# Local attention on one Trainium2 core: both key tiles of half a batch's heads in one slot

## The chip, the cores and the metric

The kernel runs on one core of one Trainium2 chip. The metric is the device time of one execution in microseconds (us), as the median of several runs. A core has TensorE (PE in the profile; PEld is its weight load), VectorE (DVE), ScalarE (ACT), GpSimd (POOL) and SyncE (SP, which issues transfers). Each engine works through its own instructions in the order in which the program issues them, and waits on semaphores for the others. Matmul results land in PSUM, which has eight banks; each bank holds 512 float32 values in each of 128 partitions.

## The reference

The whole model is a chain of sixteen blocks on a tensor of 16 x 256 tokens with 128 channels. The change touches one of them, which is used twice (second and fourth block) and has two layers, so its attention loop runs four times. What one layer computes, cut to its core:

```python
def _layer(x, wqkv, qs, ksc, wo, lg, lb, w1, b1, w2, b2):
    h = shift_token(x)
    q, k, v = jnp.split(h @ wqkv, 3, axis=-1)
    q, k, v = (to_heads(q), to_heads(k), to_heads(v))      # 8 heads of 64
    q = l2norm(q) * qs
    k = l2norm(k) * ksc
    q, k = rotary_xpos(q, k)
    o = local_attention(q, k, v)                           # windows of 64, one window back
    x = x + o @ wo
    h = shift_token(x)
    h = (h - mu) / jnp.sqrt(var + 1e-05) * lg + lb
    ...                                                    # gated feed-forward, added to x

def local_attention(q, k, v):
    ...
    sim = jnp.einsum('bhwid,bhwjd->bhwij', bq * QK_SCALE, bk)
    mask = (i < j) | (i > j + WINDOW) | (j == -1)
    sim = jnp.where(mask, -jnp.finfo(sim.dtype).max, sim)
    attn = jax.nn.softmax(sim, axis=-1)
    return jnp.einsum('bhwij,bhwjd->bhwid', attn, bv)
```

A key is seen by at most the queries of its own and the next 64 positions. With 256 tokens in two key tiles of 128, the first key tile needs 192 queries, the second 128.

## The kernel before

`local_layer` calls `local_attend` (the loop that changes) and then `local_ffn`. The four calls of `local_attend` are called loops 1 to 4 here; loops 1 and 3 are the first layer of each block, loops 2 and 4 the second. The transfers in flight during loop 1 bring weights for later stages.

Tokens are cut into 32 tiles of 128 (`NTILE`, two for each of 16 batches) and into 8 chunks of 512 (`NCH`). A unit of attention is one batch `b`, one half of the heads `hg` and one key tile `t`, which makes 64 units. The order of work is written out by hand (`manual_schedule`): slot `k` handles unit `k`, and the steps for tiles and chunks are placed at fixed offsets from it. Two slots, an even one with t = 0 and an odd one with t = 1, make one pair; a pair also takes one token tile through each of its steps. In every engine the instructions stand in the order in which the slot calls its steps.

The steps, with what each puts on the engines:

- `project` (L3385): two 128x512 matmuls for queries and keys into two banks; ACT squares each (`sq`), DVE multiplies each by the cosine and the sine table (`t1`, `t2`, four multiplies).
- `rotate` (L3403): DVE sums the squares (`ss`) and takes a maximum with a small number; POOL adds the rotated halves, two instructions.
- `unit` (L3413): ACT takes the inverse root by Ln and Exp, POOL multiplies by it (1.90 us).
- `turn` (L3421): eight transposes into two banks, which ACT copies to `qkt`, and the matmul for the values, which ACT copies to `v`.
- `score` (L3436): for t = 0, four 64-row products of 192 columns, clipped by DVE with a minimum against the table `see`, then one Exp over 768 columns (L3462). For t = 1, two mask matmuls in bf16 (an identity times the mask, started first), then four products of 128 columns added to them, then two Exp of 256 columns from PSUM (L3454).
- `weigh` (L3465), two slots later: the sums of the weights (`ones64`, into bank `pd`) and the weighted values (two halves, into bank `po`), in four column groups of 32. With t = 1, ACT forms the inverse of the sums by Ln and Exp (`rd`).
- `divide` (L3491): DVE multiplies `po` by `rd` into `ot`.
- `out` (L3501), for each chunk: four 128x512 matmuls and an addition to `z` by DVE.
- `chunk_steps` (L3514): a layer norm for each chunk in three steps (centre: matmul, ACT copy, POOL square; spread: matmul, ACT Ln and Exp; scale: DVE L543 and ACT with a bias), the shift by one token (three POOL instructions), and in the first layer the norm of `x` for those chunks that the stage before has not normed already (three of eight).

PSUM is shared as w = 3 banks (projections, turns, values, output, norms), s = 2 (scores) and o = 3 (sums). A float32 matmul is issued as two passes, so counts in the profile are twice those above. In the profile, `ps` is any PSUM bank, `w,hb` the projections, values and, after the loop, the feed-forward, `ct` the constants (identity, ones, mean matrices), and `pt` the attention weights.

## Time and profile before

| what | value |
|---|---|
| median of three runs | 4373.4 us (4373.02 to 4376.56) |
| the profiled execution | 4392.96 us |
| its span in the profile | 4391.2 us |
| granted TensorE clock over the span | 0.952 of full |
| first scores of loops 1 to 4 begin at | 140.9, 519.5, 1198.8, 1577.7 us |
| start of loop 2's first score to start of its last | 519.5 to 778.7 us |
| ACT rows `pt<-pt` 128x768 (the wide Exp) | 0.84 us each, 128 of them |
| DVE rows `pt<-ps,w` 128x384 (the minimum) | 0.55 us each, 256 of them |

A time in the profile is counted from the start of the span. "Busy" is the time in which an engine has an instruction in flight; for PE the end of a matmul is modelled, so consecutive matmuls overlap in the rows, and the starts say more than the durations. In a row of the timeline the first number is the start, the second the time until the last of a merged group ends, and the bracket holds the idle time of the engine before it and what ended it. A wait is put down to the one that came last.

### The profile page before, as it was taken

What the parts mean: (1) busy time and instruction counts of PE and PEld (TensorE: products, weight loads), DVE (VectorE), ACT (ScalarE), POOL (GpSimd) and SP (SyncE); (2) the same over time, 40 slices, a digit from 0 to 9 for tenths busy, and PEclk for the clock granted to TensorE, in tenths of its full rate; (3) what the DMA queues carried; (4) which work ended last, traced back from release to release, by engine and by line L of the source; (5) the groups of instructions that cost most, each with busy time, mean ns of one, the idle gap of its engine ahead of it and who ended that gap; (6) DMA issues with size and microseconds to landing.
All of it is one profiled execution on the core that took longest, in us unless ns stands there. A gap on an engine that the chain in (4) does not pass through costs nothing. (4 is left out here: it accounts for less than half of the span.)

```text
span 4391.2 us, 72802 instructions
## 1 busy us (share of the span) xinstructions
PE 3966.2 (90%) x28390; PEld 2202.4 (50%) x28390; DVE 2605.3 (59%) x4455; ACT 2376.1 (54%) x4549; POOL 2119.4 (48%) x1776
## 2 busy tenths in 40 slices
PE   7899999999899999995989969887999899899978
PEld 3455455466355445543975549643333344355333
DVE  4764566364366377456336643564888788386374
ACT  6665466444766456553447634445555554675442
POOL 4653355232455255315433334466998789521251
PEclk8999999999999999997999979998999999999989
DMA  1800000000000000001940029200000000000000
GB/s 59 332 1 1 11 1 1 19 1 1 19 1 1 1 3 1 1 0 49 310 162 10 15 88 326 86 18 16 1 1 1 3 1 1 15 2 18 6 0 20
DMA packets 78400, 176.36 MB, mean 40 GB/s; under 512 B 12606, under 2 KB 39108, under 8 KB 77920
## 3 DMA queue, kind: packets, MB, share of 16 engines
q1 hardware_dynamic: 65568, 148.40, 9.8%
q0 software_dynamic: 9120, 18.51, 1.2%
q8 instruction: 227, 3.72, 0.4%
q10 hardware_dynamic: 3360, 4.72, 0.3%
q14 instruction: 125, 1.02, 0.1%
HBM read 118.28 MB, written 54.20 MB: 39 GB/s over the span
## 5 line engine op out<-in xcount | busy, mean ns | idle before, releaser
L528 ACT ACTIVATE pt<-ps 128x512 f32<-128x512 f32 (+1 forms) x896 | 423.1, 537 | 408.1 <-PE ps L504 406.8
L504 PE MATMUL ps<-hb,w 128*128 128x512 f32 (+1 forms) x960 | 468.9, 623 | 5.4 <-issue 3.3
L531 DVE TENSOR_TENSOR t<-ps,tab 128x512 f32<-128x512 f32 x512 | 319.3, 683 | 196.1 <-ACT sq L528 191.3
L504 PE MATMUL ps<-w,hb 128*128 128x512 f32 (+2 forms) x896 | 415.1, 576 | 13.6 <-DVE t L531 11.3
L534 POOL TENSOR_TENSOR t<-t,ss 128x1024 f32<-128x1024 f32 x128 | 243.7, 1904 | 306.8 <-ACT ss L528 197.7
L534 POOL TENSOR_TENSOR t<-t,t 128x512 f32<-128x512 f32 x256 | 320.5, 1275 | 13.2 <-PE ps L504 10.1
L504 PEld LDWEIGHTS ps<-hb,w 128*128 128x128 f32 (+1 forms) x960 | 183.6, 196 | 273.5 <-issue 247.3
L531 DVE TENSOR_TENSOR u<-u,ps 128x384 f32<-128x384 f32 (+1 forms) x206 | 121.8, 595 | 277.8 <-ACT u L528 131.2
L534 POOL TENSOR_TENSOR nsq<-ha 128x512 f32<-128x512 f32 x112 | 123.2, 1100 | 314.1 <-ACT ha L528 297.3
L504 PE MATMUL ps<-nsq,ct 128*128 128x512 f32 x368 | 209.5, 654 | 53.9 <-POOL nsq L534 35.0
L528 ACT ACTIVATE pt<-pt 128x768 f32<-128x768 f32 (+1 forms) x160 | 169.5, 1060 | 154.6 <-DVE pt L531 154.6
L2199 POOL DMA_INDIRECT back<-y,x x142 | 139.1, 980 | 184.2 <-ACT y L528 90.2
L504 PE MATMUL ps<-qkt 64*128 64x192 f32 (+1 forms) x2048 | 216.2, 326 | 11.8 <-ACT pt L528 11.8
L504 PE MATMUL ps<-u,w 128*128 128x512 f32 (+1 forms) x448 | 218.8, 612 | 8.0 <-POOL u L534 8.0
L504 PE MATMUL ps<-ot,w 128*128 128x512 f32 x448 | 211.1, 604 | 15.2 <-POOL ot L534 6.9
L504 PE MATMUL ps<-xt,w 128*128 128x128 f32 x1704 | 219.8, 279 | 1.5 <-ACT xt L528 1.5
L504 PEld LDWEIGHTS ps<-qkt 64*128 64x128 f32 x2048 | 153.1, 188 | 133.3 <-ACT qkt L528 51.5
L504 PEld LDWEIGHTS ps<-w,hb 128*128 128x128 f32 x896 | 147.4, 192 | 139.4 <-issue 110.7
L531 DVE TENSOR_TENSOR pt<-ps,w 128x384 f32<-128x384 f32 (+1 forms) x320 | 171.2, 576 | 75.6 <-PE ps L504 72.2
L3705 POOL DMA_INDIRECT rows<-out,idx x128 | 126.4, 988 | 174.6 <-ACT out L528 125.6
L528 ACT ACTIVATE u<-ps,w 128x512 f32<-128x512 f32 x160 | 107.2, 685 | 186.3 <-PE ps L504 183.5
L531 DVE TENSOR_TENSOR pt<-pt,w 128x1024 f32<-128x1024 f32 (+1 forms) x96 | 181.1, 1886 | 42.3 <-ACT pt L528 42.3
(362 smaller groups left out, 9127.2 us busy)
## 6 DMA issues: line engine op xcount, KB each, us to landing
w<-in_moe_x SPq DMA_DIRECT2D x142, 533.0 KB
rows<-t SPq DMA_DIRECT2D x64, 520.0 KB
x<-rows SPq DMA_DIRECT2D x142, 65.0 KB
w<-in_local_f SPq DMA_DIRECT2D x8, 659.5 KB
y<-back ACTq DMA_DIRECT2D x16, 256.0 KB
y<-back SPq DMA_DIRECT2D x16, 256.0 KB
w<-in_local_f SPq DMA_DIRECT2D x4, 658.5 KB
back<-y,x POOLq DMA_INDIRECT x142
```

Source lines behind the costliest of these rows:

```text
L504: self.nc.tensor.matmul(out, lhsT, rhs, start=start, stop=stop)
L528: self.nc.scalar.activation(out, in_, func, **kw)
L531: self.nc.vector.tensor_tensor(out, a, b, op)
L534: self.nc.gpsimd.tensor_tensor(out, a, b, op)
L2199: nc.gpsimd.indirect_dma_start(views[i], bass.IndirectOffsetOnAxis(ap=x[:, C : C + 1].bitcast(I32), axis=0), y, None, bounds_check=2 * NT ...
L3705: nc.gpsimd.indirect_dma_start(views[(c * 2 + k) * 4 + t], bass.IndirectOffsetOnAxis(ap=idx[:, k, t : t + 1], axis=0), out[:, k, t], None,)
```

## The change

A slot now takes one half of a batch's heads with both key tiles. There are 32 slots, `m`, in place of 64, and one slot does what a pair did. What changes within it:

- The scores of both key tiles are formed in a row, in four banks. The masks are four bf16 matmuls of 128 columns (before: two of 256). The first two banks hold 384 columns of the first key tile and, behind them, 128 columns of the second; the third and fourth hold 128 columns each.
- The weights of the second key tile go to a tile of their own, `pu`, by four Exp of 128 columns (before: two of 256), the third and fourth bank first. They are issued after the two minima. The wide Exp of the first key tile is a step of its own, `first_weights`, issued after `turn`.
- `weigh` runs one slot later for both key tiles at once: the two halves of the values, then the sums. The sums go to the upper half of the fourth score bank of the current slot (`spare`), except in the last slot. The inverse of the sums is a step of its own, `inverse`, directly before `divide`.
- The order of a slot is score, weigh, out, turn, first_weights, rotate, inverse and divide, unit, chunk steps, project. Before, `project` and `turn` stood in different slots, `divide` and `unit` ahead of the scores, and the wide Exp directly behind the minimum.
- PSUM is shared as w = 3, s = 4, o = 1. `pt` has two buffers in place of four; `pu` has two.
- The matrices, the number of products, the tables and the transfers are as before.

```diff
-            def score(b, hg, t):
-                wide = 192 - 64 * t
+            def score(m):
+                b, hg = divmod(m, 2)
                 qt, kt = qkt[b][:, 0], qkt[b][:, 1]
-                ps = [self.bank("s"), self.bank("s")]
-                pt = p.tile([P, 2, 384], F32, tag="pt", name="pt", bufs=4)
-                if t:
+                ps = [self.bank("s") for _ in range(4)]
+                for x in (*(b[:, 384:] for b in ps[:2]), *(b[:, :P] for b in ps[2:])):
+                    self.mm(x, identb, masked, stop=False)
+
+                def product(a, i, t, out):
+                    rows, g = slice(64 * a, 64 * a + 64), 2 * hg + i
+                    wide = 192 - 64 * t
+                    nc.tensor.matmul(
+                        out, kt[rows, g, t * P : t * P + P], qt[rows, g, t * P : t * P + wide],
+                        start=False, stop=True, skip_group_check=t == 0,
+                    )
+
+                for i, t, bank, at in ((0, 0, 0, 0), (1, 0, 0, 192), (0, 1, 0, 384), (1, 1, 2, 0)):
                     for a in range(2):
-                        self.mm(ps[a][:, :T], identb, self.twice(masked), stop=False)
...
+                        product(a, i, t, ps[bank + a][:, at : at + 192 - 64 * t])
+                pt = p.tile([P, 2, 384], F32, tag="pt", name="pt", bufs=2)
+                pu = p.tile([P, 4, P], F32, tag="pu", name="pu", bufs=2)
+                for a in range(2):
+                    self.tt(
+                        pt[:, a].rearrange("p (i t) -> p i t", i=2), ps[a][:, :384].rearrange("p (i t) -> p i t", i=2),
+                        self.twice(w["see"]), ALU.min,
+                    )
+                for i, (bank, at) in enumerate(((2, 0), (0, 384))):
                     for a in range(2):
...
+                        self.act(pu[:, 2 - 2 * i + a], ps[bank + a][:, at : at + P], AF.Exp)
+                weights[m] = pt, pu
+                spare[0] = ps[3]
+
+            def first_weights(m):
+                flat = weights[m][0].rearrange("p a t -> p (a t)")
+                self.act(flat, flat, AF.Exp)
+
+            def weigh(m):
+                b, hg = divmod(m, 2)
+                pd, po = spare[0][:, T:] if m < NTILE - 1 else self.bank("s")[:, T:], self.bank("o")
+                pt, pu = weights.pop(m)
+                for half in (0, 1, -1):
+                    for t in range(2):
+                        wide = 192 - 64 * t
+                        for r in range(4):
...
+                                pu[:, r] if t else pt[:, a, i * wide : i * wide + wide],
...
+            def inverse(m):
+                pd, po = sums[m]
+                rd = p.tile([P, T], F32, tag="rd", name="rd", bufs=2)
+                self.act(rd, pd, AF.Ln)
+                self.act(rd, rd, AF.Exp, scale=-1.0)
+                sums[m] = po, rd
...
-            with self.share(w=3, s=2, o=3), self.tc.manual_schedule():
+            with self.share(w=3, s=4, o=1), self.tc.manual_schedule():
                 self.logs()
-                units = [(b, hg, t) for b in range(B) for hg in range(2) for t in range(2)]
-                for k in range(-17, len(units) + 17):
...
+                for m in range(-9, NTILE + 9):
+                    if within(m, NTILE):
+                        score(m)
+                    if within(m - 1, NTILE):
+                        weigh(m - 1)
+                    c, rest = divmod(m - 5, 4)
+                    if rest == 0 and 0 <= c < NCH:
+                        out(c)
+                    if within(m + 2, NTILE):
+                        turn(m + 2)
+                    if within(m, NTILE):
+                        first_weights(m)
+                    if within(m + 4, NTILE):
+                        rotate(m + 4)
+                    if within(m - 1, NTILE):
+                        inverse(m - 1)
+                        divide(m - 1)
+                    if within(m + 4, NTILE):
+                        unit(m + 4)
+                    chunk_steps(m)
+                    if within(m + 5, NTILE):
+                        project(m + 5)
```

In `chunk_steps` the offsets are halved: the norm of `x` at m = 4c - 9, - 8 and - 7, the shifts at 4c - 6 and 4c + 5, and the norm after the output at 4c + 6, + 7 and + 8. So of four slots in a row, one holds an output, the next a centre step, the next a spread step and the next a scale step.

## The prediction

> **What bounds the kernel now.** I read the page first, then the busy times of the four local attention loops, then the order of work on each engine inside a loop. The span, 4391.2 us, belongs to one profiled execution of 4393.0 us; the three timed runs have a median of 4373.4 us. My sum is a difference between loops of the profiled execution, and I add it to the median.

> ```profile
> span 4391.2 us, 72802 instructions
> PE 3966.2 (90%) x28390; PEld 2202.4 (50%) x28390; DVE 2605.3 (59%) x4455; ACT 2376.1 (54%) x4549; POOL 2119.4 (48%) x1776
> ```

> ```profile
> 145.00:418.00 273.00, 263.48 (x2526) 150.11 (x2528) 177.32 (x269) 173.53 (x383) 147.10 (x131) 0.99 0.24 92
> 520.00:783.00 263.00, 258.23 (x2536) 149.61 (x2535) 176.32 (x271) 169.73 (x379) 145.31 (x130) 1.00 0.01 1
> ```

> The columns are PE, PEld, DVE, ACT, POOL, clock, DMA. PE is busy for 97% to 98% of a loop, every other engine for at most two thirds. The loops hold no DMA of their own, so no step is moved past one. PE's timeline of loop 2 shows what its time goes into:

> ```profile
> 586.69 0.38 PE L504 MATMUL ps<-masked,identb 128*128 128x256 bf16 x2
> 587.00 0.71 PE L504 MATMUL ps<-qkt 64*128 64x128 f32 x8
> 587.64 0.43 PE L3478 MATMUL ps<-pt,ct 128*32 128x128 f32 x8
> 587.88 0.62 PE L3478 MATMUL ps<-pt,v 128*32 128x128 f32 x16
> 588.44 1.09 PE L508 MATMUL ps<-ct,t 128*128 128x128 f32 x8
> 589.37 1.02 PE L504 MATMUL ps<-w,hb 128*128 128x512 f32 x2
> 591.23 1.19 PE L504 MATMUL ps<-qkt 64*128 64x192 f32 x8 [0.84 <-ACT pt L528]
> 592.35 0.53 PE L3478 MATMUL ps<-pt,ct 128*32 128x192 f32 x8
> 592.70 0.83 PE L3478 MATMUL ps<-pt,v 128*32 128x192 f32 x16
> 593.47 1.98 PE L504 MATMUL ps<-w,hb 128*128 128x512 f32 x4
> 595.29 3.60 PE L504 MATMUL ps<-ot,w 128*128 128x512 f32 x8
> ```

> Read the starts. Eight output matmuls, 595.29 to 598.72, take 0.429 us each, which is 0.107 us for 128 columns and 0.161 for 192. Scores run two at a time and weighted sums four at a time, so the eight 64x128 scores should stream in 0.43 us. They took 0.64 (587.00 to 587.64). The excess appears wherever the tile shape (128*128, 64*128, 128*32) changes. In one pair of slots, all starts less all streaming come to 1.04 us for six changes. Successive 64x192 scores start 8.28, 8.28, 8.33 and 11.12 us apart (590 to 640 us): a cycle of four pairs takes 36.01 us, and 34.83 without its waits.

> **What the change removes: three shape changes in a pair.** Masks, scores, weighted sums, then 128*128 work: I count 0.50 us for the three that stay, so 0.54 us go. The two extra masks cost nothing: a mask pair is now bound by its 256 columns, and four of half the width stream as long; the nearest row, 8 to 24 column bf16 matmuls of the routing stage, starts every 25 ns, weight load included. PE's new pair is scores 1.60, weighted sums 1.77, eight transposes 0.93, values 0.86, projection 1.72: 6.88 us against 7.42. A cycle adds output 3.43 plus 0.05 and two norm matmuls of 0.86: 32.7 us. If PE stayed the bound, every cycle would gain 3 us. So I ask what waits.

> **What it adds: one closed chain over ACT and DVE.** The minimum (DVE) and the second key tile's exponentials (ACT) now read the same banks, and the next pair's minimum stands behind this pair's four rotary multiplies on DVE. These are the rows:

> ```profile
> 586.03 0.60 ACT L528 ACTIVATE sq<-ps 128x512 f32<-128x512 f32 x1 [0.28 <-PE ps L504]
> 586.66 2.48 DVE L531 TENSOR_TENSOR t<-ps,tab 128x512 f32<-128x512 f32 x4 [1.78 <-ACT sq L528]
> ```

> The square and the multiply only read one bank, yet the multiply starts 0.03 us after the square ends; the waits list this 126 times, 191.3 us. I therefore let the third and fourth new exponential wait for the minima. Both of these rows read the same columns, the new pair reads different ones, so the bounds are no wait at all and this full one; I take the full one, the nearer row.

> [...]

> From the end of the four multiplies to the end of the next four, by starts of ACT and DVE rows at 578 to 592 us: two minima 0.93, last exponential 0.19 (0.16 is my estimate from 0.27 for 256 columns and 0.48 for 512), three copies 1.43, the wide exponential 0.77, denominators Ln and Exp 0.42 + 0.32, norms Ln and Exp 0.36, first square 0.60, multiplies 2.51. Sum **7.53 us**, above PE's 6.88. Plain pairs thus take 7.53 against 7.42.

> Call D the time into a pair at which the multiplies end. The query copy ends at D + 1.75 and frees the bank that PE needs next, so a pair with a norm matmul takes D + 1.75 + 3 x 0.86 + 0.10 (restart). After an output pair D is 3.94. Centre pair: 8.37; its copy adds 0.48 to the chain, so D = 3.94 + 7.53 + 0.48 - 8.37 = 3.58. Spread pair: 8.01; Ln and Exp add 1.26, D = 4.36. Scale pair: 7.94, held by the denominators' Ln, which frees the fourth score bank.

> In the scale pair the norm's multiply (L543) now follows the division, at D + 4.80. POOL's unit multiply begins at D + 4.66, being 0.14 us behind its ACT row, and blocks it:

> ```profile
> 71.94 1.04 POOL L534 TENSOR_TENSOR nsq<-ha 128x512 f32<-128x512 f32 x1
> 71.97 1.56 DVE L543 SCALAR_TENSOR_TENSOR hb<-ha,w,nrs 128x512 f32<-128x512 f32 x1
> ```

> The same instruction takes 0.74 alone. Held until POOL's 1.90 us are over it ends at D + 7.11, then bias 0.60, squares 0.96: ACT is free at D + 8.70 = 13.06, 5.12 into the output pair. Only then come the exponentials of the third and fourth bank, +0.46 us, and the denominator matmuls write that fourth bank. PE wants them at 2.71 and gets them at 5.58: a **new wait of 2.87 us** with output, transposes, values and projection queued behind it, and ACT's copies behind those. The output pair is 10.36 + 2.87 = 13.23.

> Cycle: 8.37 + 8.01 + 7.94 + 13.23 = **37.55** against 36.01, +1.54 us. Bounds: 34.0 (neither wait) and 39.3 (plus a clock drop, below).

> **The sum.** Loops 2 and 4 have five such cycles: +7.7. The first six pairs gain 1.3 and the ramp 1.75, the turn of the third tile no longer standing ahead of the first score. The last pairs lose 4.1: without projections they used to take 6.56, 5.61 and 7.25, and now the denominators' Ln, behind the value copy and the wide exponential, holds the next scores to 7.3, 6.9 and 10.4, of which two shorter pairs give back some. Together +8.75. Loops 1 and 3 have three cycles that also norm x (39.47, 41.05, 41.05); the same walk gives 9.60 + 7.74 + 12.41 + 10.25 = 40.0, since P1's bank waits for the x copy and POOL also blocks the x multiply: -1.6. Two other cycles +3.1, ends +1.05: +2.6. All four: 2 x 8.75 + 2 x 2.6 = +22.7 us.

> Then the clock. Idle of 2.42 us stands before PE six times in loops 1 and 3:

> ```profile
> 290.83 1.40 PE L504 MATMUL ps<-nsq,ct 128*128 128x512 f32 x2 [2.42 <-ACT qkt L528]
> 290.00:294.00 4.00, 3.17 (x14) 1.64 (x18) 0.85 (x2) 2.98 (x6) 3.42 (x3) 0.69 0.02 4
> 590.00:594.00 4.00, 3.16 (x35) 1.87 (x34) 2.72 (x5) 3.71 (x11) 2.95 (x2) 1.00 0.02 4
> ```

> Four times half clock for 3.4 us followed, never after 0.84. Each costs 1.7 us. Fourteen new waits of 2.87, two thirds of them: +15.9 (bounds 0 and 34, if the x cycles' six drop too). Total +38.6: **4412 us**.

> **Rivals.** *PE stays the bound (faster).* Neither the same-bank reads nor POOL hold anything: the wait falls to 1.30, the cycle to 34.0; loops 2 and 4 gain 9 each, 1 and 3 gain 15: -48, 4325 us. For it: the 0.54 us per pair and 59% DVE; against: the 126 waits. It decides from a wait at the denominators below 1.33 us, where the cycle breaks even. *POOL comes late (no change).* The norm multiply slips in ahead, 0.14 us decides; cycle 35.98, no drops: -8, 4365 us. *The clock falls after every wait.* +34 in place of +15.9: 4430 us, more if DVE's small maximum also waits out POOL (1.22 us at 582.03 against 0.17). If the shape changes did not get cheaper, little would move: the chain, not PE, sets the pairs.

> **How the numbers follow.** Forecast 0.48 (4383 to 4430), PE bound 0.25 (4285 to 4350), no change 0.15 (4360 to 4383), every wait 0.12 (4430 to 4460). The range 4310 to 4455 leaves out about 2 in 10, mostly the lower part of the fast case; the forecast's own is 4383 to 4430. A measurement of this kernel tells about 0.2%, 8.7 us, from no change: faster 0.28 (the fast case and a piece of no change), same 0.14, slower 0.58.

> **What would show it.** Right: PE waits for ACT pt at L504 or the weighted sums once in four pairs, 2 to 3 us; DVE hb L543 near 2.4 us; score starts 37 to 38 us apart per four; ACT waiting on DVE pt. Wrong: score starts under 34 us per four, or exponentials starting while the minimum runs.

## The result, and the profile after

The changed kernel takes 4413.89 us (median of 4 runs, 4407.74 to 4417.12) against 4373.21 us for the kernel before beside it (4 runs, 4367.32 to 4376.56): a ratio of 1.0093 with a 95% interval of 1.0075 to 1.011, or 40.7 us more. The forecast was 4412, +38.6.

The totals of the page, engine by engine (busy time, share of the span, instructions):

```profile
span 4411.6 us, 73391 instructions
...
PE 3926.1 (89%) x28646; PEld 2227.0 (50%) x28646; DVE 2620.6 (59%) x4455; ACT 2366.5 (54%) x4805; POOL 2120.4 (48%) x1776
```

PE lost 40 us of busy time (3966.2 before) and the kernel became slower. So the loss is idle time in front of PE. The same view as before of one local loop (window, length, then busy time and instructions of PE, PEld, DVE, ACT, POOL, the clock, the DMA share and GB/s), here loop 2 of the changed kernel:

```profile
528.00:803.00 275.00, 250.05 (x2570) 156.56 (x2567) 181.28 (x274) 167.62 (x441) 147.97 (x131) 0.99 0.01 1
```

Here PE is busy for 91% of the stretch, where the kernel before had 98%. Measured from the first square of a loop to the first second-layer matmul of the feed-forward part behind it, the four loops went from 327.3, 312.4, 326.0 and 313.1 us to 337.0, 324.9, 334.4 and 324.8: together +42.3. What lies after the last loop took 2523.7 us in the profiled execution of before and 2505.2 in this one; nothing is changed there, and over all profiled executions it lies anywhere between 2500.8 and 2533.0. I therefore compare loops and ratios, not spans.

PE's timeline in a steady cycle of loop 2 (start, duration, engine, line, operation, tiles, shape; in brackets the idle time before it and what ended it):

```profile
704.86 0.39 PE L504 MATMUL ps<-masked,identb 128*128 128x128 bf16 x4
705.18 1.36 PE L3449 MATMUL ps<-qkt 64*128 64x192 f32 x16
...
710.87 1.98 PE L504 MATMUL ps<-w,hb 128*128 128x512 f32 x4 [0.60 <-ACT qkt L528]
712.69 0.39 PE L504 MATMUL ps<-masked,identb 128*128 128x128 bf16 x4
...
715.19 0.40 PE L3487 MATMUL ps<-pu,v 128*32 128x128 f32 x8
718.29 0.53 PE L3487 MATMUL ps<-pt,ct 128*32 128x192 f32 x8 [2.70 <-ACT pu L528]
718.64 0.40 PE L3487 MATMUL ps<-pu,ct 128*32 128x128 f32 x8
718.97 3.27 PE L504 MATMUL ps<-ot,w 128*128 128x512 f32 x7
```

Two starts of the masks, 704.86 and 712.69, are one slot apart: 7.83 us, a scale slot. In the output slot after it PE has finished the values and stands for 2.70 us before the denominators (the matmuls with `ct`, the ones), waiting for the exponentials `pu`. ACT, DVE and POOL at the same time:

```profile
709.59 0.28 ACT L528 ACTIVATE pu<-ps 128x128 f32<-128x128 f32 x1 [2.19 <-DVE pt L531]
...
716.22 0.72 ACT L528 ACTIVATE hb<-hb,w 128x512 f32<-128x512 f32 x1 [2.62 <-DVE hb L543]
716.84 1.06 ACT L528 ACTIVATE sq<-ps 128x512 f32<-128x512 f32 x2
717.80 0.44 ACT L528 ACTIVATE pu<-ps 128x128 f32<-128x128 f32 x2
```

```profile
713.27 0.69 DVE L531 TENSOR_TENSOR ot<-ps,rd 128x512 f32<-128x512 f32 x1 [1.51 <-ACT rd L528]
713.88 2.30 DVE L543 SCALAR_TENSOR_TENSOR hb<-hb,w,nrs 128x512 f32<-128x512 f32 x1
```

```profile
713.73 1.90 POOL L534 TENSOR_TENSOR t<-t,ss 128x1024 f32<-128x1024 f32 x1 [2.01 <-ACT ss L528]
```

POOL's unit multiply starts at 713.73, the norm's multiply L543 0.15 us behind it and takes 2.30 us; ACT idles 2.62 us for it, then does the bias and two squares, and only at 717.80 the exponentials that PE waits for. The waits of loop 2 (what waited, for whom, us in total, times, longest):

```profile
PE ps L3487 <- ACT pu L528: 13.7, 6, 2.7
...
ACT pu L528 <- DVE pt L531: 63.0, 57, 2.2
...
ACT hb L528 <- DVE hb L543: 14.5, 6, 2.6
```

| us, without half clock | predicted | measured |
|---|---|---|
| plain slot (no output, no norm step) | 7.53 | 7.44 to 7.57 |
| centre, spread, scale slot | 8.37, 8.01, 7.94 | 8.41, 7.99, 7.83 |
| wait at the denominators | 2.87 | 2.70 |
| output slot | 13.23 | 13.45 |
| cycle of four | 37.55 | 37.68 |
| cycle that also norms `x` | 40.0 | 40.19 |
| ramp before the first score (loop 2, against before) | -1.75 | -1.74 |
| first six slots (loop 2, against before) | -1.3 | -0.4 |
| last slots and what follows them (loop 2, against before) | +4.1 | +4.5 |

### The profile page after: what moved, and what is told of

Read it like the earlier page. It is cut to its first block, busy times and chain, and to the rows that moved or that the text cites. A ratio compares the mean times of both kernels' runs of the same rounds, so it can differ in the third digit from the quotient of the medians.

```text
span 4411.6 us, 73391 instructions
## 1 busy us (share of the span) xinstructions
PE 3926.1 (89%) x28646; PEld 2227.0 (50%) x28646; DVE 2620.6 (59%) x4455; ACT 2366.5 (54%) x4805; POOL 2120.4 (48%) x1776
## 3 DMA queue, kind: packets, MB, share of 16 engines
q14 instruction: 127, 1.04, 0.1%
## 5 line engine op out<-in xcount | busy, mean ns | idle before, releaser
L528 ACT ACTIVATE pt<-ps 128x512 f32<-128x512 f32 x640 | 339.7, 601 | 312.1 <-PE ps L504 310.8
L504 PE MATMUL ps<-hb,w 128*128 128x512 f32 (+1 forms) x960 | 471.0, 625 | 5.4 <-issue 3.3
L504 PE MATMUL ps<-w,hb 128*128 128x512 f32 (+2 forms) x896 | 410.2, 574 | 38.7 <-DVE t L531 18.0
L534 POOL TENSOR_TENSOR t<-t,t 128x512 f32<-128x512 f32 x256 | 318.7, 1267 | 181.3 <-DVE t L531 164.8
L531 DVE TENSOR_TENSOR t<-ps,tab 128x512 f32<-128x512 f32 x512 | 317.9, 682 | 101.8 <-ACT sq L528 96.3
L534 POOL TENSOR_TENSOR t<-t,ss 128x1024 f32<-128x1024 f32 x128 | 243.5, 1902 | 279.4 <-ACT ss L528 278.2
L504 PEld LDWEIGHTS ps<-hb,w 128*128 128x128 f32 (+1 forms) x960 | 184.0, 196 | 274.9 <-issue 248.9
L531 DVE TENSOR_TENSOR u<-u,ps 128x384 f32<-128x384 f32 (+1 forms) x206 | 121.7, 595 | 286.9 <-PE ps L508 183.7
L531 DVE TENSOR_TENSOR ot<-ps,rd 128x512 f32<-128x512 f32 (+1 forms) x208 | 136.5, 656 | 261.8 <-ACT rd L528 261.8
L528 ACT ACTIVATE pu<-ps 128x128 f32<-128x128 f32 x512 | 125.4, 278 | 283.9 <-DVE pt L531 260.9
L534 POOL TENSOR_TENSOR nsq<-ha 128x512 f32<-128x512 f32 x112 | 123.4, 1102 | 311.5 <-ACT ha L528 298.8
L504 PEld LDWEIGHTS ps<-w,hb 128*128 128x128 f32 x896 | 153.6, 193 | 204.7 <-issue 97.0
L504 PE MATMUL ps<-nsq,ct 128*128 128x512 f32 x368 | 206.9, 647 | 43.3 <-POOL nsq L534 38.8
L504 PE MATMUL ps<-ot,w 128*128 128x512 f32 x448 | 227.3, 645 | 13.0 <-POOL ot L534 6.8
L504 PE MATMUL ps<-u,w 128*128 128x512 f32 (+1 forms) x448 | 218.8, 612 | 8.0 <-POOL u L534 8.0
L504 PE MATMUL ps<-xt,w 128*128 128x128 f32 x1704 | 220.1, 280 | 1.5 <-ACT xt L528 1.5
L528 ACT ACTIVATE u<-ps,w 128x512 f32<-128x512 f32 x160 | 107.0, 684 | 186.1 <-PE ps L504 183.5
L531 DVE TENSOR_TENSOR pt<-pt,w 128x1024 f32<-128x1024 f32 (+1 forms) x96 | 180.6, 1882 | 43.6 <-ACT pt L528 43.4
L504 PEld LDWEIGHTS ps<-xt,w 128*128 128x128 f32 x1704 | 203.9, 194 | 2.9 <-ACT xt L528 2.9
L528 ACT ACTIVATE nrs<-ps,ct 128x512 f32<-128x512 f32 x208 | 139.6, 683 | 109.8 <-PE ps L504 102.3
```

Source lines behind the costliest of these rows:

```text
L504: self.nc.tensor.matmul(out, lhsT, rhs, start=start, stop=stop)
L528: self.nc.scalar.activation(out, in_, func, **kw)
L531: self.nc.vector.tensor_tensor(out, a, b, op)
L534: self.nc.gpsimd.tensor_tensor(out, a, b, op)
```

## The experiments

The runs were made on several chips, on which the kernel before took 4374 to 4397 us, so the ratio to it on the same chip decides; expectations in us assume 4373.

| run | edit | us (before on the same chip) | ratio and interval | cycle |
|---|---|---|---|---|
| e1_own_banks | second tile in its own banks | 4372.91 (4374.49) | 0.9996 [0.9986, 1.0005] | 35.92 |
| e2_scale_early | norm multiply early | 4366.04 (4374.49) | 0.9977 [0.9967, 0.9988] | 35.38 |
| e3_both | e1 and e2 | 4313.25 (4374.49) | 0.986 [0.9844, 0.9877] | 33.44 |
| e4_pool_later | POOL's multiply later in the program | 4414.23 (4374.49) | 1.0083 [1.0066, 1.0099] | 37.68 |
| e5_unit_late | lengths behind the norm | 4403.35 (4397.29) | 1.0013 [1.0003, 1.0023] | 36.49 |
| e6_out_first | output before denominators | 4386.91 (4397.29) | 0.9975 [0.9966, 0.9985] | 35.75 |
| e7_filled | six matmuls put into the wait | 4466.2 (4397.29) | 1.0158 [1.0141, 1.0175] | 40.13 |
| e8_three | e1, e2 and e6 | 4342.86 (4397.29) | 0.9872 [0.9855, 0.9888] | 33.56 |
| e9_filled_fit | three (two) matmuls in the wait | 4424.06 (4394.39) | 1.0059 [1.0043, 1.0076] | 37.70 |
| e10_four | e8, bias behind the Ln | 4326.78 (4394.39) | 0.984 [0.9826, 0.9855] | 33.13 |
| e11_both_again | e3 | 4337.95 (4394.39) | 0.9865 [0.985, 0.9881] | 33.44 |

Cycles are sums of four slots of loop 2 without half clock.

### Is it the shared banks? (e1)

```diff
-                for x in (*(b[:, 384:] for b in ps[:2]), *(b[:, :P] for b in ps[2:])):
-                    self.mm(x, identb, masked, stop=False)
+                for x in ps[2:]:
+                    self.mm(x[:, :T], identb, self.twice(masked), stop=False)
...
-                for i, t, bank, at in ((0, 0, 0, 0), (1, 0, 0, 192), (0, 1, 0, 384), (1, 1, 2, 0)):
+                for i, t, bank, at in ((0, 0, 0, 0), (1, 0, 0, 192), (0, 1, 2, 0), (1, 1, 2, P)):
...
-                for i, (bank, at) in enumerate(((2, 0), (0, 384))):
-                    for a in range(2):
-                        self.act(pu[:, 2 - 2 * i + a], ps[bank + a][:, at : at + P], AF.Exp)
+                for a in (1, 0):
+                    for i in range(2):
+                        self.act(pu[:, 2 * i + a], ps[2 + a][:, i * P : i * P + P], AF.Exp)
```

> The second key tile's scores move to the third and fourth bank alone, so that DVE's minima and ACT's exponentials read different banks. Theory (a closed chain over ACT and DVE sets the pairs): the exponentials start about 1.7 us into a slot and no longer 0.03 us after a minimum, plain slots fall from 7.5 to 6.9 us, centre and spread slots from 8.4 and 8.0 to 7.7, while the wait at the denominators stays at 2.7 to 2.9 us; four slots take 35.6 us in place of 37.7; total 4360 to 4380 us. Rival (the single bank for the weighted sums, and the sums' place in a score bank, are what PE waits for): slots as before the edit, 4405 to 4420 us.

Measured: plain slots 6.88, centre and spread 7.74, scale 7.00, output 13.44, and the wait of 2.69 is still there. Two plain slots on ACT and PE in e1:

```profile
538.91 1.07 ACT L528 ACTIVATE sq<-ps 128x512 f32<-128x512 f32 x2
539.86 0.78 ACT L528 ACTIVATE pu<-ps 128x128 f32<-128x128 f32 x4
```

```profile
538.12 0.38 PE L504 MATMUL ps<-masked,identb 128*128 128x256 bf16 x2
...
545.00 0.38 PE L504 MATMUL ps<-masked,identb 128*128 128x256 bf16 x2
```

All four exponentials run in one go behind the squares, with no bracket, and ACT's wait on `pt` (63.0 us in loop 2 of the changed kernel) is gone from the list of waits. The slot is 545.00 - 538.12 = 6.88 us, which is the sum that the prediction made for PE alone. So the chain through the shared banks set the pairs, and with it gone the pair is 0.54 us under the 7.42 that the prediction summed for before; that this is the three shape changes saved is its estimate, and no run tests them alone. The edit changes order and mask width with the banks: what is shown is that the wait on `pt` goes with the three together.

### The norm's multiply (e2, e3, e4, e5)

```diff
...
                     if within(m, NTILE):
                         first_weights(m)
+                    scale(m)
                     if within(m + 4, NTILE):
                         rotate(m + 4)
```

> The scale step of the norm (DVE multiply, ACT bias) is issued right behind the wide exponential and ahead of POOL's unit multiply, all else as changed. Theory: the multiply takes at most 1.3 us, ACT has the next slot's exponentials out about 2.7 us earlier, the wait at the denominators falls from 2.70 to under 0.4 us, the scale slot grows by 0.6 us because the bias now stands ahead of the denominators' Ln; four slots take 35.5 us; total 4355 to 4375 us. Plain, centre and spread slots keep 7.5, 8.4 and 8.0 us. Rival (banks of the sums): the wait stays near 2.7 us, 4405 to 4420 us.

> Both edits together. Theory: both links of the chain are gone and PE sets the pairs again: plain 6.9, centre and spread 7.7, scale 7.5, output 10.4 us, 33.4 us for four; no half clock inside the loops; total 4300 to 4325 us, below the kernel before (4373). Rival (banks of the sums): 4400 us or more.

DVE and POOL in e2:

```profile
688.98 1.12 DVE L543 SCALAR_TENSOR_TENSOR hb<-hb,w,nrs 128x512 f32<-128x512 f32 x1
```

```profile
688.28 2.95 POOL L534 TENSOR_TENSOR t<-t,t 128x512 f32<-128x512 f32 x2 [2.34 <-DVE t L531]
```

With the norm's scale step ahead of `rotate`, L543 takes 1.12 us beside POOL's two additions, no idle over 1 us is left before the denominators in the steady cycles, and the output slot falls from 13.45 to 11.14. The scale slot, expected to grow by 0.6 us, stayed at 7.83. Alone, e2 gives back more than the whole loss; with own banks as well (e3) the cycle is 33.44 (scale slot 7.00 and output slot 10.96 where I expected 7.5 and 10.4) and the kernel is 1.4% faster than before. Against the changed kernel's 1.0093, e1 is worth 0.0097, e2 0.0116 and both 0.0233: nearly a plain sum, as two separate waits give.

Why L543 was late was tried next:

```diff
...
                         unit(m + 4)
+                        if m % 4:
+                            lengths(m + 4)
                     chunk_steps(m)
+                    if within(m + 4, NTILE) and m % 4 == 0:
+                        lengths(m + 4)
```

> In scale slots alone, POOL's unit multiply is issued behind the norm's multiply; nothing else moves. Theory (POOL's multiply holds up DVE's): DVE's norm multiply takes 0.74 us in place of 2.3, the wait at the denominators falls from 2.70 to about 1.2 us, four slots take 36.1 us; total 4378 to 4392 us. Rival (POOL's multiply is only beside it, and DVE's row is long for another reason): the row stays at 2.3 us and the total at 4405 to 4420 us.

A miss: in e4 (`lengths` is POOL's unit multiply) every cycle stayed as it was.

```profile
636.10 1.90 POOL L534 TENSOR_TENSOR t<-t,ss 128x1024 f32<-128x1024 f32 x1 [2.02 <-ACT ss L528]
```

```profile
636.24 2.30 DVE L543 SCALAR_TENSOR_TENSOR hb<-hb,w,nrs 128x512 f32<-128x512 f32 x1
```

POOL still starts 0.14 us ahead of L543. The edit was empty: POOL has nothing else in its queue there, and its multiply waits for ACT's `ss`, so a later place in the program moved nothing. The test has to move what POOL waits for:

```diff
-                    if within(m + 4, NTILE):
+                    late = m % 4 == 0
+                    if within(m + 4, NTILE) and not late:
                         unit(m + 4)
                     chunk_steps(m)
+                    if within(m + 4, NTILE) and late:
+                        unit(m + 4)
```

> In every fourth pair (the scale pair) the whole key and query length step, its Ln and Exp on ScalarE included, is issued behind the norm's steps, so POOL's unit multiply can only begin after the norm's DVE multiply (L543) and its bias. If POOL's unit multiply is what holds L543: L543 falls from 2.30 to about 0.74 us, the bias comes 1.5 us sooner, and as the Ln and Exp now stand behind it (+0.45) the wait of 2.70 at the denominators falls to about 1.6 and that of 1.82 to about 0.8, cycles 37.68 -> about 36.6; with fewer half clock stretches 4375 to 4402 us. If something else makes L543 take 2.3 us: it stays at 2.3 us, the wait grows to 3.1 us and the time lies at 4415 to 4425.

DVE, ACT, POOL and PE in e5:

```profile
624.20 0.74 DVE L543 SCALAR_TENSOR_TENSOR hb<-hb,w,nrs 128x512 f32<-128x512 f32 x1
```

```profile
624.98 0.72 ACT L528 ACTIVATE hb<-hb,w 128x512 f32<-128x512 f32 x1 [1.42 <-DVE hb L543]
625.61 0.45 ACT L528 ACTIVATE ss<-ss 128x16 f32<-128x16 f32 x2
```

```profile
626.20 1.90 POOL L534 TENSOR_TENSOR t<-t,ss 128x1024 f32<-128x1024 f32 x1 [4.14 <-ACT ss L528]
```

```profile
627.42 0.53 PE L3487 MATMUL ps<-pt,ct 128*32 128x192 f32 x8 [1.50 <-ACT pu L528]
```

With POOL held back, the same L543 on the same tile takes 0.74 us, and PE's wait falls from 2.70 to 1.50. So POOL's multiply made the step late by 1.56 us. The wait falls by 1.20 and not by 1.56 because e5 also puts the unit step's Ln and Exp (0.45 us) between the norm's bias and the exponentials. A wait of 1.50 us is left as long as the norm's multiply stands behind the division; e2, which puts it ahead of both the division and POOL's multiply, leaves at most 0.33 us in the steady cycles.

### The order of output and denominators (e6)

```diff
...
-                        weigh(m - 1)
+                        weigh(m - 1, (0, 1))
                     c, rest = divmod(m - 5, 4)
                     if rest == 0 and 0 <= c < NCH:
                         out(c)
+                    if within(m - 1, NTILE):
+                        weigh(m - 1, (-1,))
```

> In each pair the value matmuls come first, then the output projection where there is one, and the denominator matmuls last; nothing else moves. If the late exponentials before the denominators are what makes the 2.70 us wait, 3.43 us of output now lie in it: no idle at the denominators, output slot about 10.4 to 11.1 in place of 13.45, cycle 34.7 to 35.4, 4350 to 4372 us, and no half clock inside the loops but in the last pairs. If PE is held by ScalarE's queue as a whole (its work between score banks), the wait moves to the transposes or to the next scores, the output slot stays at 13 us or more and the time at 4400 or above.

```profile
625.64 3.70 PE L504 MATMUL ps<-ot,w 128*128 128x512 f32 x8
629.27 0.53 PE L3489 MATMUL ps<-pt,ct 128*32 128x192 f32 x8
...
631.63 2.84 PE L504 MATMUL ps<-w,hb 128*128 128x512 f32 x6 [0.59 <-DVE ha L531]
```

The exponentials are no earlier, but now 3.43 us of output lie in front of the matmuls that need them, and the wait is gone. The output slot is 11.51, above the 10.4 to 11.1 that I expected: 0.59 us of it is a new wait further on, for the residual add (`ha`) that frees the output's bank.

### The half clock (e7, e9)

PE's timeline shows where the first wait of loop 2 lies: idle from 600.88 to 603.58.

```profile
600.48 0.40 PE L3487 MATMUL ps<-pu,v 128*32 128x128 f32 x8
603.58 0.53 PE L3487 MATMUL ps<-pt,ct 128*32 128x192 f32 x8 [2.70 <-ACT pu L528]
```

Three stretches of equal length around it in the changed kernel, read as the loop's line above (the third number from the end is the granted clock; the stretch that comes first in time is the second line):

```profile
604.43:607.85 3.42, 3.42 (x5) 1.36 (x6) 1.72 (x4) 0.55 (x2) 2.48 (x2) 0.50 0.00 0
601.01:604.43 3.42, 0.85 (x17) 0.59 (x18) 2.15 (x4) 2.02 (x5) 0.00 (x0) 1.00 0.00 0
607.85:611.26 3.41, 3.41 (x15) 1.93 (x14) 1.56 (x2) 1.09 (x2) 0.00 (x0) 1.00 0.00 0
```

PE was busy for 0.85 us of the stretch from 601.01 and the next had half clock: the output slot took 15.14 in place of 13.45, 1.69 us more. The other four waits of this loop, just as long, cost nothing more. To tell whether idle does it, PE was given work in the wait; the value bank it writes is overwritten by the values:

```diff
                 pt, pu = weights.pop(m)
+                if m % 4 == 0 and 8 <= m <= 24:
+                    for _ in range(6 if last or m in (8, 24) else 4):
+                        self.mm(po, w["wo"][:, :C], w["qkv"][:, :512])
```

> The wait itself is untouched, but PE works in it: before the value matmuls of the output pairs that wait, six 128x512 matmuls (four in those that wait 1.82 us) write into the value bank and are written over. Their results are not used. If the idle before the denominators brings the half clock stretches: none in the steady cycles, every output slot 13.45 us (x cycles 12.57), the nine stretches inside the loops go, 9 x 1.70 = 15 us, 4396 to 4404 us. If the half clock has nothing to do with the idle: stretches stay, 4410 to 4418 us. If the extra matmuls displace more than the idle, slots grow above 13.5 and the time above 4418.

```profile
644.16 5.42 PE L504 MATMUL ps<-w 128*128 128x512 f32 x12
```

The size was wrong: each of the six matmuls runs as two rows of 0.43 us, as the output's four run as eight. So 5.16 us were put into 2.70, and the output slot is 15.89 = 13.45 + 2.44. With three and two in place of six and four:

> As e7_filled, but with three extra matmuls of 128x512 before a wait of 2.70 us and two before a wait of 1.82: in e7 each of them took 0.86 us, so that six filled 5.16 us. Their results are not used. If idle of PE within one stretch of 3.413 us brings the half clock: 2.58 and 1.72 us of the waits are filled, every output slot 13.45 to 13.5 and x output slot 12.57 to 12.6, no half clock in the steady cycles, 15 us less than the changed kernel: ratio to before 1.005 to 1.007. If the half clock comes with the place in the program and not with the idle: output slots of 15.14 stay, ratio 1.009.

```profile
634.60 2.84 PE L504 MATMUL ps<-w 128*128 128x512 f32 x6
637.37 0.53 PE L3490 MATMUL ps<-pt,v 128*32 128x192 f32 x8
...
638.60 0.53 PE L3490 MATMUL ps<-pt,ct 128*32 128x192 f32 x8
```

Every output slot with a wait of 2.70 now takes 13.45 or 13.46, the granted clock from 520 to 800 us, in loop 2, is 1.00 (0.99 in the changed kernel from 528 to 803), and the loops are 14.3 us shorter in sum (1306.8 against 1321.1), close to nine times 1.70. A kernel that does more work on PE is faster (1.0059 of before, against 1.0093): in loop 2 the half clock went when the idle was filled, with the rest of the program as it was.

### The best of them (e8, e10, e11)

> Own banks for the second key tile, the norm's scale step early, and the output projection ahead of the denominators, together. If PE bounds every slot once all three waits are gone: plain 6.88, centre and spread 7.74, scale 6.9 to 7.0, output 10.4, cycle 32.9 against 33.44 with the first two alone, the waits of 1.56 us in the last pairs gone, 4290 to 4308 us. If the output slot's 10.96 is set by ScalarE or DVE and not by the denominators, the cycle stays at 33.4 and the time at 4308 to 4316.

The rival was right: the cycle is 33.56, no better than e3, and the waits of 1.56 us in the last slots, which were to go, stayed. PE's line for the scores of the output slot in e8 says why, and e10 moves the one ScalarE step that it points to (the diff is against e8):

```profile
604.79 1.79 PE L3449 MATMUL ps<-qkt 64*128 64x192 f32 x16
```

```diff
-                    scale(m)
+                    scale(m, 0)
...
                         unit(m + 4)
+                    scale(m, 1)
                     chunk_steps(m)
```

(`scale(m, 0)` is the norm's DVE multiply, `scale(m, 1)` its bias on ScalarE.)

> e8_three with one more step moved: the bias of the norm (ScalarE, 0.71 us) goes behind the denominators' Ln, which frees the fourth score bank. In e8 the scores of the output pair took 1.79 us in place of 1.36. If that bank is what holds them: scores 1.36, output slot 11.08 -> 10.65, cycle 33.13 against 33.44 in e3, and 5 to 8 us less than e3 on the same chip. If the exponentials behind the same ScalarE queue decide instead: output slot stays 11.0 to 11.1 and the time within 2 us of e3 or above it.

> The kernel of e3_both once more, beside e10_four on the same chip: cycle 33.44, ratio to before 0.985 to 0.987.

```profile
601.37 1.36 PE L3456 MATMUL ps<-qkt 64*128 64x192 f32 x16
```

Sixteen scores take 1.36 us again: the fourth score bank had been held until the denominators' Ln had read it, and the bias stood before the Ln. The output slot is 10.65, the cycle 33.13. e10 is 11.2 us below e11 on one chip where I expected 5 to 8; most of the rest lies in the last slots of loops 2 and 4, where a wait of 1.56 us is gone as well (the slot fell from 12.59 to 10.47). It beats both kernels: 0.984 of the time before.

## Why the prediction was right, point by point

**What bounds the pair.** Right, and shown: 7.53 was predicted for the chain over ACT and DVE, 7.44 to 7.57 measured, and without shared banks the pair falls to the 6.88 that the sum for PE gave. The prediction weighed no wait against the full one and took the full one; the trace has it: 57 waits of ACT on the minimum in loop 2, 63.0 us, on disjoint columns of one bank. These are waits that the profile ties to semaphores; what the chip would do without them was not tried. One reading inside the sum was wrong: the scale pair was to be held by the denominators' Ln, which frees the fourth score bank. In the trace the masks behind it start without a wait, and PE stands 0.60 us for the query copy (ACT `qkt`, 710.87), as it does in the centre and spread pairs. Their formula, with two matmuls behind the copy in place of three, gives 4.36 + 1.75 + 2 x 0.86 + 0.10 = 7.93, so that 7.94 came close to the measured 7.83 by luck.

**The norm's multiply and POOL.** Right: 2.30 us beside POOL, 0.74 without it (e5). The second rival hung on 0.14 us; POOL came 0.14 or 0.15 us ahead in all twenty of these rows in the trace.

**The wait.** Right in place and cause, 2.70 for 2.87. The first rival needed it below 1.33. What that rival described exists, but only as another kernel: with both waits removed the cycle is 33.44 (e3), where it had reckoned with 34.0.

**The loops.** Mis-sized. Without the half clock in the cycles of either side (nine stretches of 1.70 after; four of 1.58 before, 41.05 - 39.47) the loops grew by 42.3 - 15.3 + 6.3 = 33.3 us; the prediction's terms make 22.7 + 6.3 = 29.0, since it set cycles of before that held half clock against cycles of after that held none. In loop 2 the first six slots gained 0.4 in place of 1.3, five cycles cost 8.35 in place of 7.7, and the last slots 4.5 in place of 4.1: 2.0 us. Loop 4 was 1.3 us over its sum, and loops 1 and 3 together 1.0: that is the whole gap.

**The half clock.** The size came out right by luck: 15.9 predicted, 15.3 measured. Two thirds of the fourteen waits of 2.87 were to bring it; five of fourteen did, and so did four of the six waits of 1.82 in loops 1 and 3, which the sum had left at nothing. What failed is the idea of a share. In this trace half clock starts at multiples of one step of 3.413 us (below), and the cycle of 37.68 us is 11.04 such steps, so the waits of a loop move slowly against them. In loop 2 the larger part of the five waits inside one step was 2.56, 1.74, 1.61, 1.48 and 1.36 us; only the first was followed by half clock. The third rival, every wait, did not come.

## What to carry to other kernels

When work for several engines is merged into fewer and larger pieces, follow each engine's queue once around the loop: here PE became cheaper by 0.54 us a pair, and lost it because two readers came to share a bank (63.0 us of waits in loop 2) and because one multiply was moved behind another engine's long instruction (2.30 us in place of 0.74). A late operand can be hidden instead of hastened: work that doesn't need it (here the output), put ahead of the work that does, gave as much alone (e6, 0.9975) as making the operand earlier (e2, 0.9977). And moving an instruction on an engine whose queue is empty changed nothing here (e4); what had to move was what it waits for (e5).

## What the runs showed of the hardware

**The norm's multiply beside POOL.** L543 took 2.30 us when it began 0.15 us behind a POOL multiply of 1.90, 1.12 in e2 when it began 0.70 us into a POOL addition (1.27 us, the mean of these additions in the changed kernel), and 0.74 alone in e5. In both slow cases it ended 0.55 us after the POOL instruction that had begun before it, and so did the row of 1.56 us that the prediction showed (71.97 + 1.56 against 71.94 + 1.04). Where POOL was the one that began behind, by 0.14 to 0.17 us, the norm's multiply kept its 0.73 to 0.76 us in all nine such rows of the traces of before and after.
